# Four graph layers on one core: the score rows of layer 0 go through DRAM, and all places in the order are set anew

## The chip, the core and the metric

The kernel runs on one core of one Trainium2 chip. The core has five engines that run side by side: TensorE (PE, matrix products and transposes; its weight loads are listed apart as PEld), VectorE (DVE), ScalarE (ACT), GpSimd (POOL) and SyncE (SP, which here issues every DMA). The metric is the device time of one launch in microseconds (us). The time before is 3956.56 us, the median of 3 runs (3955.46 to 3960.7).

## The reference

32 graphs of N = 512 nodes with D = 256 features pass four layers; after each one, `x = layernorm(x + layer(x, adj))`. The adjacency is 0 or 1. Cut to what matters:

```python
# layer 0: 4 heads of 64
h = einsum('bnd,hde->bhne', x, W)
weight[i, j] = leaky_relu(e_src[i] + e_dst[j], 0.01)   # where adj[i, j] == 1, else -1e9
out = relu(softmax(weight) @ h + bias) + h             # then a layernorm by head
# layer 1: one head, relu scores, elu;  layer 3: one head, leaky relu 0.2
# layer 2: transformer block: 8 heads on the symmetric mask, projection, feed forward of 1024
```

In layers 0, 1 and 3 a score is a function of a sum of one number per row and one per column. Softmax over a row may be scaled by anything that depends on the row alone, so `exp(leaky_relu(s_i + d_j))` becomes, up to such a factor and one of the column, `max(exp(-0.99 s_i), exp(0.99 d_j))`. Every layer of this kind therefore needs one row of 512 numbers, `exp(-0.99 s)`, on all 128 partitions, and one column as a scalar per partition.

## The kernel before, in words

All of it is in `fast_path`; a general path runs only if a test of the row sums and the mask at the end fails. The 512 nodes of a graph lie as R = 4 blocks of P = 128 partitions. Each graph is a Python generator (`graph(b)`) that runs through stages: the edge mask (`mask`), the load of `x`, layer 0, layer 1, the symmetric mask, `qkv`, `attention`, `projection` (`attended`), `feed_forward`, `layer3`, and the store. A stage is cut into units by `yield`.

**What sets the order.** `paced` gives each unit a key, `PERIOD * b + PLACES[stage][i]`, and `heapq.merge` takes the units of all 32 graphs by the smallest key. So graphs overlap: while one is in layer 0, the one before it is in `qkv`, the one before that in feed forward or projection, and another in layer 3. TensorE executes exactly in this order (`tc.manual_schedule(engines={PE})`). The order on VectorE, ScalarE, GpSimd and SP is made by the scheduler of the framework from dependences; `in_place` ties the big mask operations (L362 `at`, L381 `a2`) to the TensorE instruction that was latest when they were recorded. Each engine's own list is fixed at build time and is executed in order.

**Buffers.** Tags carry the stage's letter (`STAGES`): `a` for edges, `x` and layers 0 and 1, `c` for feed forward and layer 3, `b` for the rest. PSUM banks: 4 for `b`, 2 each for `a` and `c`. The broadcast row `gb` has 2 buffers in `a` and 1 elsewhere; `part` tiles (the masked scores `pt`, feed forward's `ft` and others) have 7, 6 and 5. `qk` tiles have 3, `hi` and `lo` 2 each.

**Layer 0 (L393 on).** `project` multiplies the transposed `x` with the weights, to which two columns per head are appended (`h0p`, 8 products of 264 columns); ScalarE copies each block out (L332). Then ScalarE makes `ex` (L405 to L407: row factors, column factors, and the 65th column of `hv`), and VectorE makes `hv` (L398, L408). For each head `along` (L336) transposes the head's column, broadcast over 128 columns, four times (`gp`), and ScalarE copies the 128x512 result to SBUF (`gb`, L344). Four `kept` operations on VectorE (L391) make the masked scores `pt`, and 16 products with `hv` (`o0`, 65 columns, the last being the row sum) follow. Each 128x65 f32 product is two instructions in the profile. L426 and L427 divide. The head layernorm (L287 to L297), two adds and a layernorm end the layer. Layers 1 and 3 use `along` once each (`gb1`, `gb3`), and then `attend` (`o1`, `o3`).

**Around it.** `attended` transposes the attention's result (`ctp` of `cs`), divides on VectorE (L582, L586 `ctx`), transposes again (`ctp` of `ctx`, copied to `ct` by ScalarE and VectorE), and projects (`wop`, added by L607). `transposed` splits its two copies over ScalarE (L303) and VectorE (L301). In layer 3, `f` and `g` are made by L660 to L662 and `h` is multiplied by `f` (L663). Every layernorm has `bn_stats` (L265), `bn_aggr` (L266), a power on GpSimd (L269), and L270 on VectorE, and then four operations on ScalarE (L274). `qkv` makes two halves `hi` and `lo` of `q` and `k` (L502, L503) and lays them out with 64 DMAs of 64 KB per graph (L510); `attention` computes scores `s`, `exp` on ScalarE (L549), the mask on VectorE (L551), and `cp`.

Of the kernel before, what the change touches and what calls it, by code (L numbers as in the profile page):

```python
# [9 lines left out]
F32 = mybir.dt.float32  # L10
# [12 lines left out]
F32R = mybir.dt.float32r  # L23


PERIOD = 1205
PLACES = {
    "edges": [-226, -113, -5, -1],
    "x": [84],
    "mask": [1464, 1488, 1689, 1689],  # L30
    "layer 0": [
        188, 232, 373, 373, 427, 532, 536, 536, 536, 549, 603, 603, 603, 630, 637, 712, 712, 728,
        758, 758, 766, 779, 787, 791,
    ],
    "layer 1": [1024, 1057, 1078, 1123, 1135, 1135, 1151, 1276, 1299, 1366, 1385],
    "qkv": [1656, 1721, 1771, 1771, 1771, 1849, 1893, 1903, 2016, 2028],
    "attention": [
        1976, 2013, 2122, 2148, 2174, 2174, 2174, 2178, 2178, 2217, 2277, 2277, 2278, 2333, 2363,
        2405, 2452, 2475, 2493, 2527,
    ],  # L40
    "projection": [2590, 2597, 2597, 2606, 2687, 2722, 2820, 2876, 2902, 2949],
    "feed forward": [
        3051, 3062, 3135, 3169, 3169, 3196, 3221, 3327, 3328, 3357, 3381, 3419, 3447, 3483, 3512,
        3560, 3618, 3683,
    ],
    "layer 3": [3958, 3998, 4038, 4074, 4074, 4074, 4082, 4179, 4182, 4185, 4185],
}
STAGES = {"edges": "a", "x": "a", "layer 0": "a", "layer 1": "a", "feed forward": "c", "layer 3": "c"}
ALL = mybir.DependencyInfo(mybir.DependencyClass.Sync, mybir.DependencyReason.DATA)
# [22 lines left out]
def fast_path(ctx: ExitStack, tc: tile.TileContext, a: dict, out: bass.AP, bad: bass.AP):  # L72
# [8 lines left out]
    nc = tc.nc  # L81
    B, N, D = a["x"].shape
    P = 128
    R = N // P
    K = D // P
    H, _, HO = a["w0"].shape
# [13 lines left out]
    def product(what, *args, **kwargs):  # L100
        latest[0] = what(*args, **kwargs).ins.name  # L101
# [6 lines left out]
    def paced(b, name, units):  # L108

        i = 0  # L110
        while True:
            stage[0] = STAGES.get(name, "b")
            try:
                next(units)
            except StopIteration as end:
                return end.value
            yield PERIOD * b + PLACES[name][i]
            i += 1


    ident = const.tile([P, P], F32, name="ident")
# [24 lines left out]
    cols = const.tile([P, 5 * K + NF], F32, name="cols")  # L146
# [91 lines left out]

    sb = ctx.enter_context(tc.tile_pool(name="sb", bufs=1))
    ps = ctx.enter_context(tc.tile_pool(name="ps", bufs=2, space=bass.MemoryType.PSUM))  # L240
    stage = ["a"]

    def buf(shape, tag, name, bufs, dtype=F32):

        return sb.tile(shape, dtype, tag=tag + stage[0], name=name, bufs=bufs)

    def bank(name, dtype=F32):
        shape = [P, 2048 // (2 if dtype == BF16 else 4)]
        n = 4 if stage[0] == "b" else 2
        return ps.tile(shape, dtype, tag="mm" + stage[0], name=name, bufs=n)  # L250

    def part(name):

        return buf([P, N], "part", name, {"a": 7, "b": 6, "c": 5}[stage[0]])

    def all_rows(v):
        return v.unsqueeze(1).to_broadcast([P, R, D])
# [24 lines left out]
    def head_layernorm(y, eps):  # L282

        G = R * H
        yg = y.rearrange("p r (g d) -> p (r g) d", g=H)
        st = buf([P, 3, G], "lnh", "st", 2)
        nc.vector.tensor_reduce(st[:, 0, :], yg, axis=X, op=ALU.add)  # L287
        nc.vector.tensor_scalar_mul(st[:, 0, :], st[:, 0, :], 1.0 / HO)
        nc.vector.tensor_sub(yg, yg, st[:, 0, :].unsqueeze(2).to_broadcast([P, G, HO]))
        for i in range(2):  # L290
            g = slice(i * G // 2, (i + 1) * G // 2)
            sq = part("sq").rearrange("p (g d) -> p g d", d=HO)
            nc.scalar.activation(sq, yg[:, g, :], AF.Square)
            nc.vector.tensor_reduce(st[:, 1, g], sq, axis=X, op=ALU.add)
        nc.vector.tensor_scalar(st[:, 1, :], st[:, 1, :], 1.0 / HO, eps, op0=ALU.mult, op1=ALU.add)  # L295
        nc.gpsimd.tensor_tensor(st[:, 2, :], st[:, 1, :], mhalf[:, :G], op=ALU.pow)  # L296
        nc.vector.tensor_mul(yg, yg, st[:, 2, :].unsqueeze(2).to_broadcast([P, G, HO]))  # L297
# [20 lines left out]
    def project(xt, w, cols, name):  # L318

        h = buf([P, R, cols], "h", name, {"a": 2}.get(stage[0], 1))  # L320
        for r in range(R):
            yield
            p = bank(name + "p")
            for k in range(K):
                product(nc.tensor.matmul,
                    p[:, :cols],
                    xt[:, k, r * P : (r + 1) * P],
                    w[:, k, :cols],
                    start=k == 0,
                    stop=k == K - 1,  # L330
                )
            nc.scalar.copy(h[:, r, :], p[:, :cols])  # L332
        return h

    def along(cols, name):

        yield
        p = bank("gp")
        for r in range(R):
            product(nc.tensor.transpose,  # L340
                    p[:, r * P : (r + 1) * P], cols[:, r, :].to_broadcast([P, P]), ident
            )
        g = buf([P, N], "gb", name, {"a": 2}.get(stage[0], 1))
        nc.scalar.copy(g, p)  # L344
        return g
# [42 lines left out]
    def kept(name, g, edges, f):  # L388

        t = part(name)  # L390
        nc.vector.scalar_tensor_tensor(t, g, f, edges, op0=ALU.max, op1=ALU.mult)  # L391
        return t


    def layer0(x, xt, at, rd):
        h = yield from project(xt, w0, D + 2 * H, "h0")
        values = hv[:, :, :, :HO]
        nc.vector.tensor_add(  # L398
            values,
            h[:, :, :D].rearrange("p r (h e) -> p r h e", h=H),  # L400
            bias0.rearrange("p (h e) -> p h e", h=H).unsqueeze(1).to_broadcast([P, R, H, HO]),
        )
        ex = buf([P, 2, H, R], "ex", "ex0", 2)
        s, d = h[:, :, D : D + H], h[:, :, D + H :]
        nc.scalar.activation(ex[:, 0], s.rearrange("p r h -> p h r"), AF.Exp, scale=-0.99)  # L405
        nc.scalar.activation(ex[:, 1], d.rearrange("p r h -> p h r"), AF.Exp, scale=0.99)
        nc.scalar.activation(hv[:, :, :, HO], d, AF.Exp, scale=0.01)  # L407
        nc.vector.tensor_mul(values, values, hv[:, :, :, HO:].to_broadcast([P, R, H, HO]))  # L408
        y = sb.tile([P, R, D], F32, tag="y", name="y0", bufs=3)
        for hh in range(H):  # L410
            gb = yield from along(ex[:, 0, hh, :].unsqueeze(2), "gb0")
            pt = [kept("pt0", gb, at[:, j, :], ex[:, 1, hh, j : j + 1]) for j in range(R)]
            p = bank("o0")
            o = p[:, : R * HC].rearrange("p (r c) -> p r c", r=R)
            for r in range(R):
                yield
                for j in range(R):
                    product(nc.tensor.matmul,
                    o[:, r, :],
                        pt[j][:, r * P : (r + 1) * P],  # L420
                        hv[:, j, hh, :],
                        start=j == 0,
                        stop=j == R - 1,
                    )
            rdh = rd[:, hh * R : (hh + 1) * R].unsqueeze(2)
            nc.vector.reciprocal(rdh, o[:, :, HO:])  # L426
            nc.vector.scalar_tensor_tensor(  # L427
                y[:, :, hh * HO : (hh + 1) * HO],
                o[:, :, :HO],
                0.0,  # L430
                rdh.to_broadcast([P, R, HO]),
                op0=ALU.max,
                op1=ALU.mult,
            )
        nc.vector.tensor_add(x, x, all_rows(bet0))
        nc.vector.tensor_add(y, y, h[:, :, :D])
        head_layernorm(y, 1e-6)
        nc.vector.tensor_mul(y, y, all_rows(gam0))
        nc.vector.tensor_add(y, y, x)
        layernorm(y, 1e-5)  # L440
        return y
# [231 lines left out]
        return x  # L673

    ends = [0, R * H, R * (H + 1), R * (H + 1 + H2), ND]
    def load_x(b):
        xt = sb.tile([P, K, N], F32, tag="xt0", name="xt0", bufs=1)
        nc.sync.dma_start(xt, a["xt"][b].rearrange("(k p) n -> p k n", p=P))
        if b == 0:
            weights0()  # L680
        yield
        x = sb.tile([P, R, D], F32, tag="x", name="x")
        nc.sync.dma_start(x, a["x"][b].rearrange("(r p) d -> p r d", p=P))
        return xt, x

    def layer0_all(b, x, xt, at, rd):
        if b == 0:
            bcast(bet0, "bet0")
            bcast(gam0, "gam0")
        return (yield from layer0(x, xt, at, rd))  # L690
# [27 lines left out]
    def graph(b):  # L718
        yield PERIOD * b + PLACES["edges"][0]
        rd = sb.tile([P, ND], F32, tag="rd", name="rd", bufs=3)  # L720
# [29 lines left out]
    p = bank("badp")  # L750
# [645 lines left out]
```

## Time and profile before

| | before |
|---|---|
| median of 3 runs | 3956.56 us |
| the profiled execution | 3958.95 us, its span 3957.2 us |
| mean granted TensorE clock | 0.973 |
| TensorE busy | 3722.2 us, 94% of the span |
| VectorE busy | 2830.4 us, 72% |
| ScalarE busy | 1947.7 us, 49% |
| GpSimd busy | 362.0 us, 9% |
| DMA, queue of SP | 257.71 MB, 23.0% of the 16 engines' span |

How to read it: a line of groups names the source line, the engine, the operation, the tiles written and read, how many there were, the busy time with the mean of one in ns, and the idle time of the engine just before them with what ended it. L101 is the helper through which every TensorE instruction is recorded, so TensorE's groups are told apart by tiles. Ends of TensorE instructions are modelled and overlap with the next start; what one costs is read from start to start. The clock column is the share of full TensorE speed that was granted.

### The profile page before, as it was taken

Reading aid. Unit: us, or ns where it says so; the run is one execution under the profiler, and the core shown is the slowest. Engines: PE = TensorE matmul, PEld = TensorE weight load, DVE = VectorE, ACT = ScalarE, POOL = GpSimd, SP = SyncE. Lnnn points to the kernel's source line nnn. Section 1 sums busy time; section 2 is a strip of 40 time slices with the busy share of each in tenths; the row PEclk is TensorE's granted clock in tenths of the full one; section 3 lists DMA queues with packets and bytes.
Section 4 is the critical chain, followed back from the end, with each engine's and each line's share of the span. In section 5 each row is a group of like instructions: output and inputs, shape, how many; then the busy total and the mean of one; then the engine's idle time right before and its main releaser. Section 6 shows DMA issues by size and latency. Waiting matters only on the chain.

```text
span 3957.2 us, 53344 instructions
## 1 busy us (share of the span) xinstructions
PE 3722.2 (94%) x18982; PEld 2832.6 (72%) x18982; DVE 2830.4 (72%) x5626; ACT 1947.7 (49%) x4257; POOL 362.0 (9%) x266
## 2 busy tenths in 40 slices
PE   5899999999999999999999999999999999999996
PEld 4577777777777777777777777777777777777665
DVE  4667777777777777777777777777777777777753
ACT  2444455544455544455554455544455554555442
POOL 0000010010010101010101010101011101011000
PEclk6899999999999999999999999999999999999998
DMA  3222212222222222222222222222222222221110
GB/s 105 75 72 67 70 58 63 70 75 69 68 58 63 70 75 69 68 61 61 69 75 75 62 64 63 64 75 75 62 64 63 65 79 71 62 67 55 52 50 12
DMA packets 180433, 261.20 MB, mean 66 GB/s; under 512 B 36801, under 2 KB 72769, under 8 KB 180161
## 3 DMA queue, kind: packets, MB, share of 16 engines
q1 hardware_dynamic: 180160, 257.71, 23.0%
q8 instruction: 154, 2.52, 0.3%
q14 instruction: 119, 0.97, 0.1%
HBM read 106.57 MB, written 16.78 MB: 31 GB/s over the span
## 4 chain that ended last, share of the span: by engine, by line
PE 51%; DVE 17%; issue 10%; ACT 7%; POOL 7%; SPq 2%; DMA 1%; DVEq 0%; POOLq 0%; ACTq 0%
PE o L101 12%; PE f1p L101 7%; PE f2p L101 6%; DVE pr L551 5%; PE cp L101 4%; POOL rs L269 4%; PE qkp L101 3%; PE h3p L101 3%; POOL st L296 3%; PE wop L101 3%; PE h1p L101 3%; ACT y L274 2%; SPq L510 2%; DVE bn L265 2%; ACT pr L549 2%
## 5 line engine op out<-in xcount | busy, mean ns | idle before, releaser
L551 DVE TENSOR_TENSOR pr<-pr,a 128x1024 f32<-128x1024 f32 x512 | 616.7, 1216 | 220.4 <-ACT pr L549 220.2
L391 DVE SCALAR_TENSOR_TENSOR pt<-gb,ex,at 128x512 f32<-128x512 f32 x768 | 533.3, 743 | 136.3 <-ACT gb L344 136.3
L274 ACT ACTIVATE y<-y,rs 128x256 f32<-128x256 f32 x768 | 397.9, 589 | 386.0 <-DVE rs L270 385.9
L549 ACT ACTIVATE pr<-s 128x512 f32<-128x512 f32 x1024 | 542.3, 615 | 68.7 <-PE s L101 68.3
L101 PE MATMUL cp<-pr,v 128*64 128x512 f32 x2048 | 485.0, 605 | 64.7 <-DVE pr L551 64.7
L101 PEld LDWEIGHTS o<-hv,pt 128*128 128x128 f32 x4096 | 506.1, 198 | 32.6 <-DVE pt L391 16.0
L101 PE MATMUL o<-hv,pt 128*128 128x65 f32 x4096 | 507.2, 280 | 15.4 <-DVE pt L391 11.3
L101 PE MATMUL f2p<-wf,ft 128*128 128x256 f32 x2048 | 492.5, 383 | 23.2 <-ACT ft L633 22.9
L101 PE MATMUL f1p<-yt,wf 128*128 128x256 f32 x2048 | 488.7, 381 | 0.3 <-DVE yt L301 0.3
L101 PE MATMUL o<-h,pt 128*128 128x257 f32 x2048 | 482.5, 383 | 3.2 <-DVE pt L391 3.1
L101 PEld LDWEIGHTS o<-h,pt 128*128 128x128 f32 x2048 | 381.1, 190 | 97.0 <-ACT y L274 23.5
L101 PEld LDWEIGHTS f2p<-wf,ft 128*128 128x128 f32 x2048 | 379.1, 190 | 95.6 <-ACT ft L633 46.8
L633 ACT ACTIVATE ft<-f1p,cols 128x256 f32<-128x256 f32 x512 | 216.7, 479 | 454.5 <-PE f1p L101 454.5
L269 POOL TENSOR_TENSOR rs<-rs,mhalf 128x4 f32<-128x4 f32 x192 | 234.9, 1224 | 2146.4 <-DVE rs L268 2092.5
L101 PEld LDWEIGHTS f1p<-yt,wf 128*128 128x128 f32 x2048 | 382.4, 190 | 52.3 <-issue 0.8
L101 PEld LDWEIGHTS cp<-pr,v 128*64 128x64 f32 x2048 | 127.9, 137 | 346.0 <-DVE pr L551 150.3
L101 PE MATMUL s<-qk 128*128 128x512 f32 x1024 | 359.1, 456 | 1.8 <-ACT pr L549 1.7
L265 DVE BATCH_NORM_STATS2 bn<-y 128x6 f32<-128x256 f32 x768 | 295.8, 409 | 3.5
L101 PEld LDWEIGHTS s<-qk 128*128 128x128 f32 x1024 | 187.0, 190 | 97.9 <-issue 52.7
L101 PE MATMUL qkp<-xt,wqkv 128*128 128x512 f32 x512 | 232.2, 596 | 0.9 <-DVE xt L301 0.9
L296 POOL TENSOR_TENSOR st<-st,mhalf 128x16 f32<-128x16 f32 x32 | 120.9, 3779 | 978.3 <-DVE st L295 978.3
L567 ACT COPY cs<-cp 128x512 f32<-128x512 f32 x128 | 74.5, 582 | 259.6 <-PE cp L101 259.6
(129 smaller groups left out, 4500.0 us busy)
## 6 DMA issues: line engine op xcount, KB each, us to landing
qk<-hi SPq DMA_DIRECT2D x1024, 64.0 KB, 2.0
qk<-lo SPq DMA_DIRECT2D x1024, 64.0 KB, 2.0
adjt<-in_adjt SPq DMA_DIRECT2D x64, 512.0 KB, 3.3
adj<-in_adj SPq DMA_DIRECT2D x64, 512.0 KB, 3.4
xt<-in_xt SPq DMA_DIRECT2D x32, 512.0 KB, 3.6
x<-in_x SPq DMA_DIRECT2D x32, 512.0 KB, 3.6
out<-y SPq DMA_DIRECT2D x32, 512.0 KB, 3.1
wf<-in_w1t SPq DMA_DIRECT2D x1, 1024.0 KB, 7.9
```

What stands on the lines that cost most here:

```text
L101: latest[0] = what(*args, **kwargs).ins.name
L265: nc.vector.bn_stats(st[:, r, :], y[:, r, :])
L269: nc.gpsimd.tensor_tensor(rs[:, 1, :], rs[:, 0, :], mhalf[:, :R], op=ALU.pow)
L274: nc.scalar.activation(y[:, r, :], y[:, r, :], AF.Identity, bias=rs[:, 2, r : r + 1], scale=rs[:, 1, r : r + 1],)
L296: nc.gpsimd.tensor_tensor(st[:, 2, :], st[:, 1, :], mhalf[:, :G], op=ALU.pow)
L391: nc.vector.scalar_tensor_tensor(t, g, f, edges, op0=ALU.max, op1=ALU.mult)
L510: nc.sync.dma_start(t[hh // 2][g * DH : (g + 1) * DH, s, hh % 2, :].bitcast(F32), src[hh * DH : (hh + 1) * DH].bitcast(F32),)
L549: nc.scalar.activation(t[:, i, :], s, AF.Exp, scale=QSCALE)
L551: nc.vector.tensor_mul(t, t, edges)
L567: nc.scalar.copy(t, cp)
L633: nc.scalar.activation(ft[:, f, :], p[:, f, :], AF.Relu, bias=bf1[:, ff + f : ff + f + 1])
```

## The change

Layer 0 no longer calls `along`. A new `rows_of` transposes all 16 columns `ex[:, 0]` (4 heads x 4 blocks) at once into 16 partitions, ScalarE copies them to SBUF, and one DMA writes the 16x128 block to a DRAM tile. `over` reads the 512 numbers of one head back onto all 128 partitions with a DMA of partition step 0. The reads of heads 0 and 1 are recorded before the loop over heads; the read of head `hh + 2` after the `kept` operations of head `hh`, whose buffer it takes (tag `gb`, 2 buffers, as before). Layers 1 and 3 keep `along`. `PERIOD` and all places are set anew, ten times finer (1205 becomes 12054), so that units of different stages stand in another order.

```diff
-PERIOD = 1205
+PERIOD = 12054
 PLACES = {
...
-        188, 232, 373, 373, 427, 532, 536, 536, 536, 549, 603, 603, 603, 630, 637, 712, 712, 728,
-        758, 758, 766, 779, 787, 791,
+        3030, 3674, 5154, 5154, 5513, 5713, 5713, 6363, 6733, 6733, 6733, 6733, 6733, 6823, 6823,
+        7123, 7223, 8237, 8237, 8397, 8697, 8777, 8907, 8989, 9029,
...
+    dram = ctx.enter_context(tc.tile_pool(name="dram", bufs=1, space=bass.MemoryType.DRAM))
...
+        rows = yield from rows_of(ex[:, 0].rearrange("p h r -> p (h r)"), "gr0")
+        gbs = []
+        for hh in range(2):
+            yield
+            gbs.append(over(rows, hh, "gb0"))
         for hh in range(H):
-            gb = yield from along(ex[:, 0, hh, :].unsqueeze(2), "gb0")
+            gb = gbs[hh]
             pt = [kept("pt0", gb, at[:, j, :], ex[:, 1, hh, j : j + 1]) for j in range(R)]
+            if hh + 2 < H:
+                yield
+                gbs.append(over(rows, hh + 2, "gb0"))
             p = bank("o0")
...
+    def rows_of(cols, name):
+
+        m = cols.shape[1]
+        yield
+        p = bank("gp")
+        product(nc.tensor.transpose, p[:m, :P], cols, ident)
+        g = buf([m, P], "gr", name, 1)
+        nc.scalar.copy(g, p[:m, :P])
+        rows = dram.tile([m, P], F32, tag="rows", name=name + "d", bufs=2)
+        nc.sync.dma_start(rows, g)
+        return rows
+
+    def over(rows, i, name):
+
+        g = buf([P, N], "gb", name, 2)
+        src = rows[i * R : (i + 1) * R]
+        nc.sync.dma_start(g, bass.AP(tensor=src.tensor, offset=src.offset, ap=[[0, P], [1, N]]))
+        return g
```

## The prediction

> **What bounds the kernel now.** I read the page first: its totals, its slices and its groups by shape. TensorE is busy 94% of the span, in nearly every slice 9 tenths or more; the next engine is at 72%.
>
> ```profile
> span 3957.2 us, 53344 instructions
> PE 3722.2 (94%) x18982; PEld 2832.6 (72%) x18982; DVE 2830.4 (72%) x5626; ACT 1947.7 (49%) x4257; POOL 362.0 (9%) x266
> ```
>
> The run is a steady beat: 32 graphs, one after the other at the same offset. The table of stretches, cut where the first `ctp` transposes of three successive graphs begin, shows two kinds of beat (columns: stretch, length, busy time and count of PE, PEld, DVE, ACT, POOL, clock, DMA share, GB/s).
>
> ```profile
> 1973.03:2090.24 117.21, 112.92 (x594) 86.44 (x592) 88.02 (x177) 60.69 (x133) 11.29 (x8) 1.00 0.24 68
> 2090.24:2209.13 118.89, 114.59 (x593) 87.84 (x592) 87.94 (x177) 60.70 (x133) 11.29 (x8) 0.99 0.24 67
> 2209.13:2328.03 118.90, 114.60 (x593) 87.69 (x592) 87.92 (x177) 60.80 (x133) 11.29 (x8) 0.99 0.24 67
> ```
>
> The same work takes 117.2 us in one beat and 118.9 in two; mean 118.33. Where do 1.69 us come from? The same table in steps of 3.4 us around the place where the beat is thinnest:
>
> ```profile
> 2094.83:2098.24 3.41, 1.71 (x9) 1.10 (x9) 3.19 (x12) 2.61 (x6) 0.15 (x1) 1.00 0.00 0
> 2098.24:2101.66 3.42, 3.42 (x14) 3.01 (x13) 2.30 (x6) 2.18 (x5) 1.01 (x1) 0.50 0.22 78
> ```
>
> After a stretch in which TensorE was half idle, 3.41 us ran at clock 0.50: that is 1.7 us. The idle beforehand is TensorE waiting for VectorE's `ctx` (timeline of PE, columns start, length, work, idle before and releaser; this beat had no dip):
>
> ```profile
> 1978.39 0.38 PE L101 MATMUL ctp<-ident,ctx 128*128 128x128 f32 x2
> 1979.03 0.33 PE L101 MATMUL ctp<-ident,ctx 128*128 128x128 f32 x1 [0.26 <-DVE ctx L586]
> 1980.80 0.77 PE L101 MATMUL ctp<-ident,ctx 128*128 128x128 f32 x5 [1.45 <-DVE ctx L586]
> 1981.40 0.60 PE L101 MATMUL xt3p<-ident,y 128*128 128x128 f32 x4
> 1981.84 1.95 PE L101 MATMUL h0p<-w,xt 128*128 128x264 f32 x8
> ...
> 1989.72 0.65 PE L101 MATMUL gp<-ident,ex 128*128 128x128 f32 x4
> 1990.21 0.60 PE L101 MATMUL xt2p<-ident,y 128*128 128x128 f32 x4
> ```
>
> So a beat is 113.0 us of TensorE work, 4.2 us of named stalls (`ctx` 1.71, `f2p` 0.50, `cp` 0.84 and 1.11) and, in two of three, a 1.7 us dip. The wall is TensorE's order, with small stalls where an engine in turn is late.
>
> [...] dips are 3.413 us long, on one grid. [...] every dip in the steady part follows a window in which `ctp` and `xt3p` transposes stood almost alone; with 5 or more of the `h0p` instructions in it there is none. [...] No DMA of this kernel before reads back what one wrote.
>
> **The change, part by part**, against the profiled span (3957.2; run 3958.95, median of the runs 3956.56, so 2 us apart).
>
> *Removed.* Four `gp` groups of layer 0 per graph: 128 groups of 4 transposes. A group holds TensorE 0.44 us from start to next start (timeline: 0.43 to 0.49): 128 x 0.45 = 57.6 us. Also 128 copies `gb<-gp` at 0.583 us: 75 us of ScalarE, which at 49% bounds nothing here; I count nothing for it. What it hides behind is TensorE's order.
>
> *Added on TensorE.* One transpose of 16 columns per graph, no wider than one of `gp`'s four: 0.12 us x 32 = 4 us. Net 1.68 us per beat, 54 us in all. On ScalarE 32 small copies (about 0.25 us, by the 0.2 us of the 16-column `ex`).
>
> *Added as DMA.* Per graph one 8 KB write and four broadcasts of 256 KB. The broadcast has a twin: `a<-in_a` has the same form, 3.1 us from issue to landing at its quickest, which was the one issued alone at 49.80. The write has none; the 64 KB `qk` pieces take 2.0, 512 KB of `out` 3.1: I take 2.0, bounds 1.5 and 3.0. The round trip is thus 5.1 us (4.6 to 6.5) after the copy, where the old route was a copy of 0.58. Traffic: 33.5 MB on 261 MB, with the engines at 23%: room.
>
> *Order on SP.* In the built order each graph's queue reads second `adj` half, `xt`, the write, three broadcasts, an `adjt` half, the fourth broadcast, then the 64 `qk` pieces. The write waits for nothing late: `adj` and `xt` leave at about 9.8 and 10.5 us after the beat's start (in the old beat 9.4 and 10.8) and 1 MB is through before the write is issued at 13.4. The third broadcast waits until VectorE has used the first, the fourth for the second, at about 31.4; all `qk` pieces stand behind that. They started at 28.2 in the old beat, will start at 32. First user `s` comes at 62, 24 pieces at 0.63 us plus 2.0 landing give 49: 13 us to spare, cost nothing; without that cover each us late would be one us.
>
> *Moved, and the new stalls.* The new TensorE order, costed with start-to-start times of the 117.2 us beat, from its start (0):
> 1. `ctp` of the cs tiles together, then `h0p`, end at 5.3; two `ctx` transposes. VectorE now does the third and fourth `rd`/`ctx` without two `bn_stats` between: last `ctx` at 7.0 instead of 7.7. TensorE waits 0.53 + 0.88, from start to start, where before it waited 0.42 + 1.66: gain 0.7. Then 5 `ctx`, all 8 `xt3p` together, `h0p` ends at 10.3.
> 2. The last `h0p` copy on ScalarE stands behind four `y` normalizations (2.0 us), which wait for POOL: `ex` at 12.5. `wop` and two `h3p` are through at 12.0: TensorE waits 0.54 for the new transpose. New.
> 3. `wop`, six `h3p`: 16.15. Layer 3's `gp` now follows `h3p` directly; before, `wop` (0.87) stood between and covered the copy and `ex` (profile: `h3p` end 2107.75, `gp` 2108.61). Stall 0.85. New.
> 4. `gp`, four `wop`, two `xt2p` groups: 20.05, ready for `o0`. VectorE: `h` times `f` (L663 of before) now stands ahead of the first head's four `kept` and ends at 18.4 (it needs layer 3's last copy). The round trip: copy ends 13.3, write 15.4, broadcast 18.5. Both arrive together, so `kept` runs 18.5 to 21.1 and the fourth tile is missed by 0.4 to 0.5 us. New.
> 5. VectorE then has layer 3's four `kept`, two adds, two `bn_stats`, one L381, the copy of `xt2`: 27.1. `qkp` wants it at 26.6. Stall 0.5. New.
>
> `qkp` ends at 31.4 where the quick beat had 30.68, though 0.78 us of transposes is gone by then; the two remaining `gp` give back 0.90 later, one `o3` may wait 0.2. A beat without a dip: 117.21 + 0.74 - 0.90 + 0.2 = 117.25. The 1.68 us saved are spent on waits.
>
> *The dips.* The stretch without ordinary matmuls (from `h0p`'s end at 5.3 to the next `h0p` at 8.5) is 3.2 us; it was 3.45. Stepping the grid with a beat of 117.3 I get dips in half to two thirds of the beats. A dip now costs 1.2 to 1.7, since step 2's wait swallows 0.5 of it. Mean beat 117.25 + 0.6 x 1.35 = 118.06, against 118.33: 30 beats x 0.27 = 8 us. The first graph, alone on the chip: the first head comes some 5 us later (the broadcast stands behind weights that took 7.9 us to land), the next three each save the 1.06 + 1.60 of `gp` and its wait: -2 us. Sum 3957 - 8 - 2 = **3947**, by the runs' median the same within 2 us.
>
> **Rivals.**
> *The saving stays (3880 to 3925, say 3905).* If ScalarE and VectorE, with 75 us less to copy, bring `ex` and `xt2` earlier than I reckon, the stalls of 2 and 5 (1.0 us) shrink to half and dips become rare: 117.25 - 0.5 = 116.75, x 30 = -47 us. For it: VectorE idles 26% and the `ctx` wait does shrink. Against: steps 2 to 5 are chains of dependent work, not load.
> *The round trip is late: slower (3985).* Place: the first head's `kept`. It decides once the broadcast lands over 0.1 us after 18.4; each us more is 30 us. With the write at 3.0 and some queueing, 1.2 us late: +36, and the half-rate `o0` behind a longer wait may cost dips of its own. For it: write and read are strictly in series and no spare time is left. Against: SP is free, and the traffic low.
> *The `qk` pieces come late (3975 or more)*: needs 13 us of delay on SP. Weak.
> That the change does not do what it says is excluded by the built order: 512 transposes are gone.
>
> **How the numbers follow.** Forecast case 0.50 (own range 3928 to 3968: the beat sure to 0.5 us), saving stays 0.22, round trip late 0.24, `qk` 0.04. To leave out 2 in 10, half of the first rival's low part and the tail of the late cases go: 3908 to 3988. About 0.2% (8 us, so 3949 and 3965) is what can be told from no change. Faster: 0.25 of the forecast case and 0.22 = 0.47. Same: 0.16 and 0.02 = 0.18. Slower: 0.09 + 0.22 + 0.04 = 0.35.
>
> **What would show it.** Right: TensorE busy some 50 us less while its idle time grows; waits of `gp` for `ex` of layer 0 and layer 3, of `o<-hv,pt` for `pt`, of `qkp` for `xt2`'s copy; broadcasts landing in 3.1 us; the `ctx` wait near 1.1 as recorded. Wrong: write plus read far from 5.1; beats without dips; `pt` waiting for DMA by over a microsecond; a wait in the `s` or `cp` part that I took as unchanged.

## The result and the profile after

The changed kernel takes 3945.12 us (median of 7 runs, 3943.77 to 3946.89) against 3958.04 for the kernel before on the same chips (7 runs): ratio 0.9968, 95% interval 0.9957 to 0.9980. The forecast was 3947. It is right in its number, and wrong in two of its terms, which by luck cancelled. The rest of this part and the runs are about that.

Profiled, the span is 3942.9 us, 14.3 less than before. First line of the page and its totals, and the row of the DMA issues for the new broadcast (size, then median us from issue to landing):

```profile
span 3942.9 us, 52309 instructions
PE 3667.3 (93%) x18502; PEld 2750.3 (70%) x18502; DVE 2814.5 (71%) x5626; ACT 1869.5 (47%) x4161; POOL 377.3 (10%) x266
...
gb<-gr0d SPq DMA_DIRECT2D x128, 256.0 KB, 3.3
```

TensorE is busy 54.9 us less, which is what the removed transposes were to give. That agreement is an accident, as the table of stretches shows, cut again at the first `ctp` of four successive graphs (columns as before: stretch, length, busy time of PE, PEld, DVE, ACT, POOL, clock, DMA share, GB/s):

```profile
1848.21:1966.10 117.89, 112.48 (x579) 84.76 (x578) 87.39 (x177) 58.29 (x130) 11.88 (x8) 1.00 0.27 76
1966.10:2083.98 117.88, 112.47 (x578) 84.76 (x577) 87.38 (x177) 58.29 (x130) 11.88 (x8) 1.00 0.27 77
2083.98:2201.88 117.90, 112.48 (x579) 84.75 (x578) 87.41 (x177) 58.28 (x130) 11.88 (x8) 1.00 0.26 76
```

These beats are alike, and none has a clock dip: 117.89, where before they were 117.21 without a dip and 118.9 with one. (Three others of the steady part are 0.1 to 1.1 us longer, with no dip either.) By the trace's record of the granted clock, 18 dips (61.4 us at half clock; each 3.413 us long, all on one grid of that step) lay between 430 and 3600 us before, and none after. So the beat without dips has become *longer*, by 0.68 us, and the dips are gone. Before, TensorE's busy time in a dip-free beat was 112.92, now 112.47: 0.45 less, not 1.68. The page's 54.9 us are, by an estimate from these figures, some 31 us of dips (busy at half clock) and some 14 us of beats (0.45 x 32); the remaining 10 would lie outside the steady part.

The chain in the beat's start, on PE's timeline (start, length, work, in brackets the idle time before and who ended it):

```profile
1971.45 0.38 PE L101 MATMUL ctp<-ident,ctx 128*128 128x128 f32 x2
1972.16 0.33 PE L101 MATMUL ctp<-ident,ctx 128*128 128x128 f32 x1 [0.33 <-DVE ctx L595]
1973.10 0.77 PE L101 MATMUL ctp<-ident,ctx 128*128 128x128 f32 x5 [0.60 <-DVE ctx L595]
...
1977.22 1.03 PE L101 MATMUL h3p<-w3g,xt 128*128 128x258 f32 x4
1979.55 0.28 PE L101 MATMUL gp<-ident,ex 128*16 128x128 f32 x1 [1.30 <-ACT ex L406]
1979.66 1.03 PE L101 MATMUL wop<-wo,ct 128*128 128x256 f32 x4
1980.53 2.78 PE L101 MATMUL h3p<-w3g,xt 128*128 128x258 f32 x12
1984.01 0.65 PE L101 MATMUL gp<-ident,ex 128*128 128x128 f32 x4 [0.70 <-ACT ex L669]
...
1987.10 0.83 PE L101 MATMUL o<-hv,pt 128*128 128x65 f32 x6
1988.16 3.12 PE L101 MATMUL o<-hv,pt 128*128 128x65 f32 x26 [0.23 <-DVE pt L392]
...
1992.91 5.65 PE L101 MATMUL qkp<-xt,wqkv 128*128 128x512 f32 x12
1998.39 1.90 PE L101 MATMUL o<-h,pt 128*128 128x257 f32 x8
```

The `ctx` wait shrank as reckoned (1.71 to 0.93 as recorded). The new transpose waits 1.30 for `ex`, layer 3's `gp` 0.70, the first narrow products 0.23. The whole path of the rows is kinder than reckoned: the write is issued at 1980.16, the first broadcast, which waits for it, at 1981.53 (1.37 us for the write instead of 2.0; 1.36 to 1.40 in 24 of the 32 graphs, up to 3.2 in the others):

```profile
1980.16 0.33 SPq L694 DMA_DIRECT2D gr0d<-gr  x1
1981.53 0.83 SPq L701 DMA_DIRECT2D gb<-gr0d  x2
```

With 3.1 to 3.3 us it lands by about 1984.8, and VectorE's first `kept` (L392) starts only at 1985.38, when it is through with L672. The round trip had about 0.6 us to spare. VectorE's timeline:

```profile
1984.23 1.23 DVE L672 TENSOR_TENSOR h<-h 128x1024 f32<-128x1024 f32 x1 [1.40 <-ACT h L671]
1985.38 4.72 DVE L392 SCALAR_TENSOR_TENSOR pt<-gb,ex,at 128x512 f32<-128x512 f32 x7
```

Why 1.30 at `ex`, when 0.54 was reckoned? The chain goes back to POOL's power for layer 1's normalization (L270; L269 before). Timelines of POOL and VectorE, after:

```profile
1974.74 1.92 POOL L270 TENSOR_TENSOR rs<-rs,mhalf 128x4 f32<-128x4 f32 x1 [3.91 <-DVE rs L269]
```

```profile
1974.51 0.15 DVE L269 SCALAR_TENSOR_TENSOR rs<-mv 128x4 f32<-128x4 f32 x1
1974.58 1.22 DVE L382 TENSOR_TENSOR a<-at,adj 128x1024 uint8<-128x1024 uint8 x1
1976.70 0.16 DVE L271 SCALAR_TENSOR_TENSOR rs<-mv,rs 128x4 f32<-128x4 f32 x1 [0.90 <-POOL rs L270]
```

and in the kernel before, POOL and then VectorE:

```profile
1981.11 1.01 POOL L269 TENSOR_TENSOR rs<-rs,mhalf 128x4 f32<-128x4 f32 x1 [3.35 <-DVE rs L268]
```

```profile
1981.17 1.22 DVE L381 TENSOR_TENSOR a<-at,adj 128x1024 uint8<-128x1024 uint8 x1
1982.31 0.15 DVE L270 SCALAR_TENSOR_TENSOR rs<-mv,rs 128x4 f32<-128x4 f32 x1
```

The same operation on 128x4 numbers takes 1.01 us when it begins 0.06 ahead of VectorE's mask, and 1.92 when it begins 0.16 behind it. So it is in all 28 graphs of either trace in which the two overlap: 1.01 at 0.05 to 0.09 ahead in the kernel before, 1.92 at 0.16 to 0.17 behind in the changed one. POOL takes 0.91 us longer when it is second; VectorE's mask takes 1.22 us either way. By what means the one holds up the other the traces don't show.

### The profile page after: what moved, and what is told of

It reads as the page before. It is cut to its first block, busy times and chain, and to the rows that moved or that the text cites. A ratio compares the mean times of both kernels' runs of the same rounds, so it can differ in the third digit from the quotient of the medians.

```text
span 3942.9 us, 52309 instructions
## 1 busy us (share of the span) xinstructions
PE 3667.3 (93%) x18502; PEld 2750.3 (70%) x18502; DVE 2814.5 (71%) x5626; ACT 1869.5 (47%) x4161; POOL 377.3 (10%) x266
## 4 chain that ended last, share of the span: by engine, by line
PE 43%; DVE 25%; issue 10%; POOL 7%; ACT 7%; DMA 0%; POOLq 0%; DVEq 0%; ACTq 0%
PE o L101 12%; PE f2p L101 6%; PE f1p L101 6%; PE qkp L101 5%; POOL rs L270 5%; DVE pr L560 4%; DVE pt L392 4%; PE cp L101 4%; ACT y L275 3%; POOL st L297 3%; PE h1p L101 3%; DVE bn L266 3%; PE h3p L101 2%; PE s L101 2%; PE vp L101 1%
## 5 line engine op out<-in xcount | busy, mean ns | idle before, releaser
L392 DVE SCALAR_TENSOR_TENSOR pt<-gb,ex,at 128x512 f32<-128x512 f32 x768 | 530.5, 743 | 79.5 <-PE o L101 43.7
L270 POOL TENSOR_TENSOR rs<-rs,mhalf 128x4 f32<-128x4 f32 x192 | 251.1, 1308 | 2202.2 <-DVE rs L269 1752.3
L101 PE MATMUL qkp<-xt,wqkv 128*128 128x512 f32 x512 | 241.3, 605 | 3.5 <-DVE xt L302 1.5
L435 DVE RECIPROCAL rd<-o 128x4 f32<-128x4 f32 x128 | 22.0, 179 | 268.0 <-PE o L101 268.0
```

The source lines that it names most:

```text
L270: nc.gpsimd.tensor_tensor(rs[:, 1, :], rs[:, 0, :], mhalf[:, :R], op=ALU.pow)
```

## The experiments

Two theories were set against each other first. **T**: the dips come from windows in which too few columns are streamed, transposes counting as much as products; the change gains because its order has no such window. **P**: transposes don't count, as the prediction assumed; no trace had shown it. And beside both: is the gain from the rows by DRAM, or from the places?

In the table, the ratio of each run is to runs of the kernel before made together with it (their medians lie between 3954.6 and 3958.0). *Half clock* is the time at clock 0.50 by the trace's record, in the whole span and between 430 and 3600 us; it is that of the profiled execution, which isn't always near the median (3981 with the mask later, 3944 with its nine transposes, 3950 with `gp` behind `wop` and eight). *Without dips* is the profiled span less half of the whole half-clock time: an estimate, which takes each dip to cost half its length, as in the kernel before (118.90 - 117.21 = 1.69 us for 3.41); where TensorE waits within a dip it may cost less.

| kernel | us, median | ratio to before | half clock, us | without dips |
|---|---|---|---|---|
| before | 3958.04 | 1 | 215.7 / 61.4 | 3849 |
| changed | 3945.12 | 0.9968 (0.9957 to 0.9980) | 154.4 / 0 | 3866 |
| places alone | 4139.39 | 1.0457 (1.0442 to 1.0471) | 391.8 / 208.2 | 3944 |
| rows alone | 4081.21 | 1.0315 (1.0295 to 1.0336) | 414.5 / 225.3 | 3872 |
| before, 8 transposes in the wait | 3921.95 | 0.9910 (0.9895 to 0.9926) | 146.2 / 0 | 3847 |
| before, 4 products in the wait | 3928.38 | 0.9920 (0.9906 to 0.9933) | 151.0 / 0 | 3852 |
| changed, mask later | 3988.79 | 1.0084 (1.0071 to 1.0097) | 238.2 / 85.3 | 3861 |
| changed, gp behind wop | 3969.32 | 1.0038 (1.0024 to 1.0053) | 215.9 / 61.4 | 3863 |
| changed, one more hop | 4100.12 | 1.0366 (1.0353 to 1.0380) | 365.4 / 180.9 | 3915 |
| rows alone, 8 + 8 transposes | 4007.89 | 1.0137 (1.0123 to 1.0152) | 254.5 / 95.6 | 3878 |
| gp behind wop, 8 transposes | 3944.81 | 0.9969 (0.9957 to 0.9981) | 163.4 / 13.7 | 3867 |
| mask later, 9 transposes | 3951.45 | 0.9985 (0.9978 to 0.9991) | 154.3 / 17.1 | 3865 |
| rows alone, 8 + 16 transposes | 3964.93 | 1.0016 (1.0008 to 1.0025) | 157.5 / 10.2 | 3881 |

**Work in the wait.** In `transposed`, on the kernel before:

```diff
             for r in range(R):
+                if name == "ct" and k == 0 and r == R - 1:
+                    for _ in range(8):
+                        product(nc.tensor.transpose, p[:, r * P : (r + 1) * P], ident, ident)
                 product(nc.tensor.transpose,
```

> The kernel before, with eight transposes of the identity put into the wait for the last ctx (about 0.9 us of TensorE that nobody needs, in a wait of 1.45). It adds work and leaves nothing out. Theory T ([...] the dips come from the share of a window in which columns are streamed): the dips of the steady part go, and 20 of them at 1.7 us are worth 34: about 3925, with the clock near 0.98 or more. Rival P (only ordinary products count): the dips stay, the time stays at 3957, or is a few us longer. Rival N (the dips have nothing to do with the wait): 3957, dips as before.

The other has four `nc.tensor.matmul(..., ident, ident, start=True, stop=True)` in the same place: eight instructions, about 0.9 us by an estimate from 0.112 us for a product's instruction of 65 columns and 0.109 for a transpose of 128.

> As with the eight transposes, but four ordinary products of identity and identity of 128 columns in the same wait (about 0.9 us at the slower rate of these). It adds work and leaves nothing out. Theory T and rival P both say that the dips go: about 3925. Rival N: 3957 with dips as before. Together with the eight transposes: both fast means that transposes count, products alone fast means that they do not.

Both are faster than before, by 36 and 29 us, with no dip left in the steady part. PE's timeline of the first shows the eight transposes in the wait for `ctx`, then its table of stretches:

```profile
1962.28 0.33 PE L101 MATMUL ctp<-ident,ctx 128*128 128x128 f32 x1 [0.26 <-DVE ctx L589]
1962.45 1.04 PE L101 MATMUL ctp<-ident 128*128 128x128 f32 x8
1964.06 0.77 PE L101 MATMUL ctp<-ident,ctx 128*128 128x128 f32 x5 [0.57 <-DVE ctx L589]
```

```profile
1839.07:1956.29 117.22, 113.80 (x602) 87.27 (x601) 88.06 (x177) 60.63 (x133) 11.28 (x8) 1.00 0.24 68
1956.29:2073.51 117.22, 113.79 (x602) 87.26 (x601) 88.05 (x177) 60.64 (x133) 11.28 (x8) 1.00 0.24 68
```

Each beat is the dip-free one of before, to 0.01 us, though each has 0.87 us more work. P falls: adding transposes, and nothing else, ends the dips. (These two runs alone don't tell whether they count fully or in part; the count over all traces further down does.) What thinned the windows of the kernel before was the wait of 1.71 us beside the transposes, not the transposes.

This is also the fastest kernel of the case: the old rows and the old places, with useless work in one wait, beat the change by 23 us.

**Places alone, rows alone.** The first has all places of the changed kernel (layer 0's list fitted to 24 entries) and none of its rows; the second the rows of the changed kernel and the old places (layer 0's list stretched to 25). In diffs against the kernel before:

```diff
-PERIOD = 1205
+PERIOD = 12054
...
     "layer 0": [
-        188, 232, 373, 373, 427, 532, 536, 536, 536, 549, 603, 603, 603, 630, 637, 712, 712, 728,
-        758, 758, 766, 779, 787, 791,
+        3030, 3674, 5154, 5154, 5513, 6733, 6733, 6733, 6733, 6733, 6823, 6823, 7123, 7223, 7223,
+        8237, 8237, 8397, 8697, 8697, 8777, 8907, 8989, 9029,
     ],
```

> All places of the changed kernel, but the score rows still made as before: four gp groups and four copies per graph. Theory A (the saving is TensorE's 1.68 us of gp per beat; the new places only arrange waits): TensorE's busy time goes back up by about 54 us to 3722, part of it fills waits that the changed kernel has, and the time is 3965 to 3995, slower than both. Rival B (the new order alone brings the gain, by ending the clock dips of the steady part, and the DRAM rows bring nothing): at most 3947. In both, if the order of the ctp, h0p and xt3p groups is what ends the dips, the clock in the steady part is 1.00 here too; if the dips come back, it was something else.

```diff
-        188, 232, 373, 373, 427, 532, 536, 536, 536, 549, 603, 603, 603, 630, 637, 712, 712, 728,
-        758, 758, 766, 779, 787, 791,
+        188, 232, 373, 373, 427, 447, 447, 495, 532, 536, 536, 536, 536, 603, 603, 603, 630,
+        712, 712, 728, 758, 766, 779, 787, 791,
...
+        rows = yield from rows_of(ex[:, 0].rearrange("p h r -> p (h r)"), "gr0")
```

> The rows by DRAM, with the places of the kernel before (the layer's list stretched by one entry). Theory A (rows save TensorE 1.68 us per beat; the places decide how much is spent on waits and dips): TensorE busy 3668, the ctx wait of 1.71 and the dips of the kernel before still there, one new wait of o for pt: 3935 to 3960, say 3947. Rival B (the gain is in the places alone): 3957 or more. Rival C (the old places were the better ones and the new ones threw the saving away): about 3905.

No theory foresaw this: 4139 lies outside both ranges of the first run, and 4081 fits only the open "3957 or more" of rival B, whose gain from the places alone the first run refutes. Each half alone is far slower than both kernels. The table's last two columns say why, for the rows alone for the most part: without dips they would be near 3872, where the kernel before would be near 3849. For the places alone dips are 88 us of the 182; the other 95 stand in beats that are longer without them. TensorE's named waits sum to 6.7 us per beat there, against 4.3 before (5.4 in the changed kernel); what makes up the rest is open. With the rows alone some dips still follow the `ctx` wait (in none of the runs with the new places does one stand there); most stand at a place to which only the prediction's rival of a late round trip had pointed. PE's timeline of the rows alone, then its stretches at the same place, in steps of 3.41 us:

```profile
2052.05 0.44 PE L101 MATMUL o<-hv,pt 128*128 128x65 f32 x2 [0.77 <-DVE pt L392]
2052.72 0.44 PE L101 MATMUL o<-hv,pt 128*128 128x65 f32 x2 [0.23 <-DVE pt L392]
2053.38 0.44 PE L101 MATMUL o<-hv,pt 128*128 128x65 f32 x2 [0.23 <-DVE pt L392]
2054.04 4.14 PE L101 MATMUL o<-hv,pt 128*128 128x65 f32 x26 [0.23 <-DVE pt L392]
```

```profile
2051.99:2055.40 3.41, 2.67 (x18) 2.25 (x19) 3.41 (x7) 0.00 (x0) 0.00 (x0) 1.00 0.06 22
2055.40:2058.82 3.42, 3.42 (x18) 3.33 (x18) 2.45 (x5) 0.00 (x0) 0.00 (x0) 0.57 0.32 73
2058.82:2062.23 3.41, 3.41 (x9) 2.68 (x9) 2.20 (x4) 0.59 (x1) 0.00 (x0) 0.50 0.39 136
```

Layer 0's products stream 65 columns each. When TensorE gets to them early, it takes each `kept` tile as VectorE delivers it: two instructions, 0.23 us of waiting, two instructions. A 65-column instruction takes 0.112 us from start to start (median in both traces), about as long as a transpose of 128 columns (0.109), so such a run is thin even without waits. Behind this stretch the clock is 0.57 and then 0.50, at half for two windows of 3.413 us: 3.4 us lost for waits of 0.7 within the run. The changed kernel at the same place had one such wait of 0.22 or 0.23 in 25 of the 27 beats between 430 and 3600 us (PE's timeline in the first part), three and four waits of 0.06 to 0.23 in the other two, and no dip in any. The places alone dip behind three such waits (0.16 to 0.23) at later heads, and behind a `cp` wait of 1.98. New theory **D**: what the change does well, besides the shorter `ctx` wait, is that TensorE comes to the narrow products late enough.

**Taking the changed kernel's own waits away.** Theory D says that the waits at `gp` are not only lost time. Two edits take them away.

```diff
-    "mask": [16160, 16210, 17540, 18380],
+    "mask": [16160, 16700, 17540, 18380],
```

> The changed kernel with one place moved: the first half of the symmetric mask (L382, 1.22 us of VectorE) now stands behind L271 and the copy of xt3 instead of between L269 and L271. Theory A (POOL's power for layer 1's normalization, L270, takes 1.92 us instead of 1.01 because VectorE begins the mask beside it, and this holds up the y normalizations, the last h0p copy, ex and the new transpose): L270 back at 1.0, the wait of gp for ex down from 1.29 to about 0.4, the beat from 117.89 to about 117.1, 3915 to 3928. Rival B (the next chain takes it over: the xt3 copy, the mask and the wop additions now stand before L672 on VectorE, so o waits longer for pt): L270 is short, but the beat stays at 117.7 or more: 3938 to 3948. Rival C (the clock dips come back with a beat of another length): over 3950.

```diff
-    "layer 3": [40334, 40334, 41526, 41766, 41766, 41886, 41942, 42909, 42969, 42999, 42999],
+    "layer 3": [40334, 40334, 41526, 41766, 41766, 41886, 42020, 42909, 42969, 42999, 42999],
```

> The changed kernel with layer 3's gp group put behind the two wop groups that follow it, as before the change. Theory A (what sets the first o of layer 0 is VectorE's chain of L672 and four kept, which does not start with gp): the wait of gp for ex (0.70) goes, the wait of o for pt grows by as much, and the time stays within 8 us of 3945. Rival B (each wait of TensorE costs its own): 0.7 x 30 = 21 us less, about 3924.

The first settles what half of the 1.30 comes from. With the mask behind L271, POOL's timeline:

```profile
1873.55 1.01 POOL L270 TENSOR_TENSOR rs<-rs,mhalf 128x4 f32<-128x4 f32 x1 [3.90 <-DVE rs L269]
```

L270 is back at 1.01 (theory A so far), and the wait for `ex` goes to 0.65. But the beat without a dip stays at 117.6 to 117.8 (rival B by its number), with three waits of 0.23 at the narrow products, and the dips come (rival C): 3989, slower than before. It moves a transfer as well: the 512 KB of the second half of the adjacency are now issued 1.8 us ahead of the 8 KB write, which then takes 2.8 us (issue at 1878.32, first broadcast at 1881.14) instead of 1.37. That, and not VectorE's list as rival B had it, is what sets the first `kept` here. VectorE's waits for the broadcast between 430 and 3600 us (sum, times, longest), in the changed kernel and then with the mask moved:

```profile
DVE pt L392 <- DMA gb<-gr0d: 1.7, 2, 1.1
```

```profile
DVE pt L392 <- DMA gb<-gr0d: 9.5, 19, 1.7
```

So this run shows what makes the wait for `ex` long, but not what the beat would gain if that alone were mended.

The second is the cleaner one. Its dip-free beat is 117.87, the changed kernel's to 0.02 (theory A in its mechanism: VectorE's L672 and the four `kept` set the first `o`, and 0.70 at `gp` is only waited elsewhere). Yet it is 24 us slower, outside theory A's 8 us, through 12 dips of one or two windows. A wait moved from before a group of wide instructions into a run of narrow ones has a price that no sum of waits shows.

**Giving the time back as work.** Ahead of the first `o` of layer 0, eight useless transposes on the kernel with `gp` behind `wop`, nine on the one with the mask later:

```diff
                 for j in range(R):
+                    if hh == 0 and r == 0 and j == 0:
+                        for _ in range(8):
+                            product(nc.tensor.transpose, p[:, 384:512], ident, ident)
                     product(nc.tensor.matmul,
```

> The changed kernel with layer 3's gp group behind wop (3969 as measured), and eight transposes of the identity, 0.87 us of TensorE that nobody needs, ahead of the first o product of layer 0 in each graph. Theory D (o then starts when the four kept are all but done, so that its narrow products run without the three waits of 0.23, and the clock dips that follow them are gone): slower work makes it faster, beat 117.9 throughout, 3942 to 3950. Rival N (the dips have another cause in the moved group): 3969, or 26 more by the added work.

> The changed kernel with the mask moved (3989 as measured), and nine transposes of the identity ahead of the first o product of layer 0. Theory D: the dips go, the beat is its dip-free 117.7 throughout, 3935 to 3946. Rival N: 3989 or more.

The first, on PE's timeline:

```profile
1984.58 1.04 PE L101 MATMUL o<-ident 128*128 128x128 f32 x8
1985.46 0.82 PE L101 MATMUL o<-hv,pt 128*128 128x65 f32 x6
1986.51 3.12 PE L101 MATMUL o<-hv,pt 128*128 128x65 f32 x26 [0.23 <-DVE pt L392]
```

The narrow products stand as in the changed kernel, with one wait, and so does the time: 3944.81 against 3945.12. Adding 0.87 us of work to each graph made the kernel 24 us faster. The second gains 37 us in the same way and ends at 3951, some 5 above the expected range; its 21 runs spread from 3943.6 to 3961.5. The profiled one is the fastest, and even it has some dips left (17.1 us at half clock). D stands in both.

**The rows alone, filled.** Eight transposes in the `ctx` wait of the rows-alone kernel, and eight, then sixteen, ahead of the first `o`.

> The rows by DRAM with the places of the kernel before, which gave 4081, now with eight transposes of the identity in the wait for ctx and eight more ahead of the first o product of layer 0 in each graph. It adds work and leaves nothing out. Theory T (its 124 us are clock dips in the two thin stretches, ctx and the first o products; a beat without dips is about 117.9): most dips go, beat 118 to 119, 3945 to 3975. Rival N (the time is in the waits themselves and the clock only follows): about 4080.

> The rows by DRAM with the places of the kernel before, eight transposes in the ctx wait as in the run that gave 4008, and sixteen instead of eight ahead of the first o product of layer 0: that run still had three waits of 0.23 among the narrow products. Theory D: with o starting at about 20.4 us of the beat at most one such wait is left, and the dips go: beat 117.9 to 118.1, 3942 to 3955. All of the 134 us by which the rows alone stand above that is then clock dips. Rival N: 4008, or up to 26 more by the added work.

With 8 + 8 the dips after `ctx` are gone, those at the narrow products are not (three waits of 0.23 are left there; 95.6 us at half clock): 4008, above the range of T. With 8 + 16 all but 10 us are gone, and so are 116 us of the 124 by which the rows alone were slower than before. The expected 3942 to 3955 was missed by 10 us: the added transposes are not all hidden (without dips the estimate is 3881, against 3872 for the rows alone).

**The round trip.** One more hop between the write and the broadcasts:

```diff
         rows = dram.tile([m, P], F32, tag="rows", name=name + "d", bufs=2)
-        nc.sync.dma_start(rows, g)
+        first = dram.tile([m, P], F32, tag="first", name=name + "e", bufs=2)
+        nc.sync.dma_start(first, g)
+        nc.sync.dma_start(rows, first)
```

> The changed kernel with one more hop in the round trip: the 8 KB of rows are written to one DRAM tile and copied to a second, from which the broadcasts read. It delays every broadcast by the time of one small DMA, 1.3 to 2.0 us. In the changed kernel the first broadcast lands some 0.6 us before the kept that needs it can start. Theory A (slack of 0.6, then one for one, as the prediction had it): 0.7 to 1.4 us per beat, 3966 to 3987. Rival B (a longer wait among the narrow o products brings clock dips, each 1.7 us or more): over 4000. Rival C (there is more slack than I see): 3945.

SP's queue shows what the hop takes (1936.35 to 1938.45, 2.1 us; in other beats 1.85 to 2.1), and PE's timeline what became of it:

```profile
1936.35 0.49 SPq L696 DMA_DIRECT2D gr0d<-gr0e  x1
1938.45 6.83 SPq L703 DMA_DIRECT2D gb<-gr0d  x3
```

```profile
1942.99 0.44 PE L101 MATMUL o<-hv,pt 128*128 128x65 f32 x2 [0.90 <-DVE pt L392]
1943.65 0.44 PE L101 MATMUL o<-hv,pt 128*128 128x65 f32 x2 [0.23 <-DVE pt L392]
1944.32 0.44 PE L101 MATMUL o<-hv,pt 128*128 128x65 f32 x2 [0.23 <-DVE pt L392]
1944.98 5.39 PE L101 MATMUL o<-hv,pt 128*128 128x65 f32 x26 [0.23 <-DVE pt L392]
```

Without dips it loses 49 us by the estimate, 1.5 us per beat: about the hop less the slack of 0.6, as theory A has it. The agreement is rough, for in this build VectorE also takes three of layer 3's `kept` before those of the first head (eight follow L672 from 1940.20 on, 0.66 apart, and the first `o` starts when the fourth is done). With dips it loses 155 (rival B): the 26 products that took 3.12 us take 5.39. At the prediction's 30 us for each us of lateness it would have been 45.

**One count over all thirteen traces.** This is an estimate from TensorE's records. A 257-column instruction takes 0.216 us from start to start (median in both traces), so a column streams in 0.84 ns. Lay the dips' grid of 3.413 us over each trace from 430 to 3600 us, take the windows at full clock, and add up in each the columns of all instructions, transposes like products (those of `s` and `cp` at half: two `cp` instructions of 512 columns begin 0.007 us apart and the next two 0.43 after them, and those of `s` come 0.32 apart in the mean, where 512 columns at 0.84 ns would be 0.43). Call their streaming time, as a share of the window, the streamed share. Each of the 182 windows that a dip follows has less than 0.395; of the 11610 others all but 7 have more. With transposes at half weight the best dividing line misplaces 93 windows, and with transposes left out it finds next to none of the dips. So theory T holds with full weight, and D is one case of it: 65 columns are 0.055 us of streaming in 0.112, and a few waits of 0.23 bring such a run under the line. The changed kernel's thinnest window has 0.402. It is free of dips by a hair, which fits that moving one unit brings them back.

## Why the prediction was right in its number and wrong in its terms

- **The beat without a dip, 117.25: wrong, it is 117.89, by step 2.** The new transpose begins 13.45 us into the beat (1979.55 - 1966.10), reckoned 12.5, and the rest of the chain keeps that distance: layer 3's `gp` at 17.91 (17.0), the first `o` at 21.00 (20.05), the end of `qkp` at 32.29 (31.4). Later 0.25 of it is regained; `f2p`, for one, waits 0.16 instead of 0.50.
- **Where the 1.68 went.** The instructions are gone, but the idle time by the table rose by 1.12 (117.88 - 112.47 = 5.41 against 117.21 - 112.92 = 4.29), and 1.23 more (1.68 - 0.45) went into groups that look busy. The mean distance from one instruction's start to the next, named idle time taken off, between 400 and 3500 us, against the filled kernel before, which has no dips either: `h3p` 218 to 238 ns (x16 per graph: 0.32 us), `qkp` 429 to 446 (0.27), `s` 296 to 306 (0.30), `f2p` 216 to 220 (0.24), 1.13 together. Of this 0.48 is waiting that the view gives to the wrong side: since ends are modelled, the last instruction before a wait looks 0.16 us longer. The last `h3p` before each of the two `gp` takes 0.38 us in this count, every other one 0.22; the last `qkp` before its wait for `xt2` likewise. What the rest waits for the profile doesn't name and no run tried.
- **Step 1, the `ctx` wait: right** (0.33 + 0.60 as recorded).
- **Step 2, `ex` at 12.5 and a wait of 0.54: mis-sized, 1.46 from start to start (1.30 named).** The step took POOL's power as 1.0 us, as before. In the new order VectorE begins its mask 0.16 us ahead of it instead of 0.06 behind, and it took 1.92. The run with the mask moved shows that this is half of the wait; 0.65 named (0.81 from start to start) is left there. Its beat is only 0.05 to 0.33 shorter, but its write is longer too, so what this wait alone costs the beat stays open.
- **Step 3, `gp` of layer 3: right** (0.70 named, 0.86 from start to start, for 0.85).
- **Step 4, `o` for `kept`, 0.4 to 0.5: right** (0.23 named, 0.39 from start to start: 1.06 us for six instructions of 0.112). L672 does stand ahead of `kept` and bounds it. The round trip was taken as landing at the same moment (5.1 us); it lands 0.6 earlier because the write took 1.37 for 2.0.
- **Step 5, `qkp`, 0.5: near.** `qkp` takes 5.48 us to the next start, 0.33 more than in the dip-free beat before.
- **The SP queue, cost nothing: right.** The `qk` pieces begin 32.4 us into the beat (reckoned 32), and no wait for them grew.
- **The dips, 0.6 of the beats at 1.35: wrong, none.** The step that failed is the assumption by which they were counted, that a window without ordinary products dips; it was the author's, and no trace had shown it. The changed kernel still has 3.13 us of transposes and waits between two `h0p` groups (1971.45 to 1974.58), its beat of 117.89 is no multiple of 3.413 and so passes over many positions of the grid, and no beat dips. The run with eight transposes shows that filling the wait is enough, and the count over all traces that a transpose weighs as much as a product of its columns.
- Together: +0.64 per beat from waits, -0.81 from dips, times 30: +19 and -24. The error of the sum was 2 us, which is luck.
- **The rival of a late round trip: priced too low.** Its place and its point were right; 1.5 us of lateness are worth 155 us here, not 45, because the wait falls among narrow products. The prediction mentioned dips there and gave them no number. The rival in which the saving stays had ScalarE and VectorE come early; where they did come earlier, as with the mask moved, the result was slower.

## What to carry to other kernels

TensorE is busy 93 to 94% of the span here, and time at half clock cost 31 us in the steady part of the kernel before and 113 with the rows alone (an estimate: half of 61.4 and of 225.3). Where a trace shows such dips, look for each stretch of their length (3.413 us here) in which TensorE is half idle or runs narrow products (here, one with a streamed share below about 0.4, by the estimate above), and ask what the change does to the waits there before counting the instructions that it saves. A wait ahead of wide work can be cheaper than no wait there and three small ones in a run of narrow products (with `gp` behind `wop`, 24 us); filling such a wait with useless transposes is a three-line test of whether it costs clock (36 us gained in the kernel before). And when two halves of a change are measured alone, expect no sum: places alone cost 182 us, rows alone 124, together they gained 13.

## What the hardware showed beyond that

- Eight 128x128 transposes of 0.11 us each in a wait of 1.45 us ended all 18 dips of the steady part; four ordinary products did as well.
- A window of 3.413 us was followed by one at half clock when its streamed share, transposes counted like products, was below about 0.395 (an estimate from thirteen traces, 7 exceptions in 11792 windows).
- Runs of 65-column products (0.112 us an instruction from start to start) kept the full clock in all 27 steady beats of the changed kernel, in 25 of them with one wait of 0.22 or 0.23 us. Behind a run with three such waits the clock was 0.57 and then 0.50 in steps of 3.41 us with the rows alone, and 0.58 and then 0.50 with `gp` behind `wop`.
- A POOL operation on 128x4 numbers took 1.01 us where it began 0.05 to 0.09 us ahead of VectorE's mask of 1.22 us, and 1.92 where it began 0.16 to 0.17 behind it (28 graphs each).
- An 8 KB write to DRAM was followed by the read that depends on it 1.36 to 1.40 us after its own issue in 24 of 32 graphs; 1.85 to 2.1 for a copy from DRAM to DRAM, 2.8 for the write where a 512 KB read was issued 1.8 us earlier. A row of 2 KB read onto all 128 partitions landed in 3.3 us (median).
